# An LSTM whose input part arrives by accumulating DMAs: the bias under each step's tile written by ScalarE in place of a DMA

## The chip, the cores and the metric

The kernel runs on one core of one Trainium2 chip. The metric is the time of one execution on the device in microseconds, as the median over runs; lower is better. One further execution was taken with the hardware profiler on, and all rows of the profile come from that one.

## The reference

A batch of 32 sequences of 512 steps with 512 features goes through one LSTM layer of width 512, and the layer's output is added to its input. All numbers are fp32.

```python
xW = jnp.einsum('ntd,dg->ntg', x, Wx) + b          # 32 x 512 x 2048
def step(carry, xw_t):
    prev_h, prev_c = carry
    a = xw_t + prev_h @ Wh
    i, f, o = sigmoid(a[:, :H]), sigmoid(a[:, H:2*H]), sigmoid(a[:, 2*H:3*H])
    g = tanh(a[:, 3*H:])
    next_c = f * prev_c + i * g
    next_h = o * tanh(next_c)
    return (next_h, next_c), next_h
out = x + hs                                        # hs: all next_h
```

The bias `b` is a vector of 2048 numbers, one for each gate column, and it is not zero.

## The kernel before

The work has two halves that run side by side for nearly the whole time. The recurrence must go step by step: `h_part(k)` multiplies the state `ht` of the step before by `Wh` into two PSUM banks (`gates`), and `cell(k)` makes the new state from them. The input part `x @ Wx` doesn't depend on the recurrence, so its matmuls fill the time in which TensorE would wait for the cell.

**The input part.** The first 48 steps and the last 16 are made in simpler ways. The 448 steps between go in 14 blocks of 32. A block's product is made as 26 smaller products of sums of its rows with sums of blocks of `Wx` (the tables `A_OPS`, `B_OF`, `C_OPS`), and each of the 26 again as seven matmul groups (`product`). The sums of `Wx` lie in DRAM (`keep_a`, `keep_b`) and are fetched for each product into two rings of SBUF tiles, `wa` (3 buffers) and `wb` (4 buffers), by `fetch(v)`, lines 918 and 922; the rows of `x` for a block are fetched there too, four row loads of 512 KB for each block (line 214). ScalarE and VectorE move and add the PSUM results (`evacuate`, `finish_product`, lines 493 to 507, 617, 629, 645), and `store` (line 529) writes the finished blocks to DRAM in four pieces each, without the bias.

**A step's own tile.** For each step `t` from 8 to 495 a tile `xw[t]` of 128 x 512 floats (256 KB; a ring of four) is first filled with the bias, which stands in SBUF as `bias_sb` in the same shape. This is `fill_bias(t)`, line 715, and it is done by a plain DMA from SBUF to SBUF. Then `load_xw(t)`, line 719, issues a DMA on GpSimd that adds the stored product from DRAM onto the tile. Last, ScalarE copies the tile into the two banks ahead of the step's matmuls: `seed_first` (line 742) and `seed_last` (line 748).

**The order** is written out by hand, each engine's instructions in the order in which the program names them, and TensorE's, ScalarE's, VectorE's, GpSimd's and SyncE's queues each run in that order:

- In step `k` the loop first issues the load of residual rows (every second step), then `fill_bias(k + 4)` and `load_xw(k + 3)`.
- Then it puts `h_part(k)` on TensorE.
- Then come `evacuate`, the sums that are due, the matmuls `products(v)` with `v = k + 4`, and `fetch(v)`. So on ScalarE the copies of the evacuation stand ahead of the cell.
- Then comes `cell(k)`: ScalarE's three activations (lines 794 to 796), VectorE's products (797 to 799), ScalarE's tanh (800), VectorE's product and transpose (801, 802), which give `ht`. `put_step` adds the residual on GpSimd (line 855), and every second step SyncE issues the output's DMA (line 858).
- Last come the seeds for the steps after: `seed_first(k + 2)` and `seed_last(k + 1)`.

From step 469 on (`HALVES`), the cell and its matmuls go in two halves (`h_halves`, line 771, `cell_halves`, lines 816 to 842), with the same fill and load.

So SyncE's queue holds the fills, the fetches of `wa` and `wb`, the rows, the stores and the outputs, one behind the other. GpSimd's queue holds the accumulating DMAs and the residual's additions, one behind the other. A DMA that has to wait for something holds what stands behind it in its queue.

Of the kernel before, what the change touches and what calls it, by code (L numbers as in the profile page):

```python
# [40 lines left out]
END = HEAD + NSB * PER  # L41
# [131 lines left out]
def kernel(  # L173
# [9 lines left out]
    nc = tc.nc  # L183
# [19 lines left out]
    bias_sb = const.tile([P, G * P], F32, name="bias_sb")  # L203
# [5 lines left out]
    rows, xw, stored = {}, {}, {}  # L209
# [42 lines left out]
    def t_sums(i):  # L252
        w, t = raw[i], tt_[i]
        return [
            lambda: nc.vector.tensor_sub(t[:, 0::3], w[:, 1::2], w[:, 0:2]),
            lambda: nc.vector.tensor_sub(t[:, 1], w[:, 3], t[:, 0]),
            lambda: nc.vector.tensor_sub(t[:, 2], w[:, 2], t[:, 1]),
        ]
# [30 lines left out]
    def push_factors():  # L289
        v = nc.vector  # L290
        made, ops, done = {}, [], []

        def outer(n, how, a, b, part):
            if n not in made:
                made[n] = ring(n, f"make_{n}")

            def source(u):
                if part == 2:
                    return tt_[u] if u < 8 else made[u - 8][1]
                if u < 8:  # L300
                    return raw[u][:, 0:1] if part == 0 else raw[u][:, 2:4]
                return made[u - 8][0][:, 0:1] if part == 0 else made[u - 8][0][:, 1:3]

            (v.tensor_add if how == "add" else v.tensor_sub)(source(8 + n), source(a), source(b))

        for n in range(R):
            if streamed(n) and len(B_OF[n]) == 1:
                i = B_OF[n][0][0]
                ops.append((0, lambda n=n, i=i: keep(n, (raw[i][:, 0:1], raw[i][:, 2:4]), tt_[i])))
        for op in B_OPS:  # L310
            if isinstance(op, int):
                n = -1 - op
                ops.append((0, lambda n=n: keep(n, (made[n][0][:, 0:1], made[n][0][:, 1:3]), made[n][1])))
            else:
                for part, columns in ((0, C), (1, 2 * C), (2, 4 * C)):
                    ops.append((columns, lambda op=op, part=part: outer(*op, part)))
        for i, (columns, fn) in enumerate(ops):

            def go(fn=fn):
                fn()  # L320
                done.append(fn)

            push(2 + (START - 6) * i // len(ops), columns, go, lambda _, i=i: len(done) == i)
# [151 lines left out]
    def products(v):  # L475
        for late, ss in ((4, (4,)), (2, (7,)), (0, (1,)), (1, (6,)), (0, (5,)), (1, (5,)), (3, (2, 3))):
            job = jobs.get(v - late)
            for s in ss if job else ():
                if s != 5 or job.w5 == v:
                    product(job, s)  # L480
                if s == 4:
                    job.release()
# [183 lines left out]
    def direct(t, bank, qs=range(4), cols=slice(0, 512)):  # L666
        i, a = divmod(t, ROW)
        for q in qs:
            k, e = divmod(q, 2)
            for j in range(NJ):  # L670
                nc.tensor.matmul(  # L671
                    flat(bank)[j * B : (j + 1) * B, cols],
                    rows[i][:, a, q],
                    raw[NJ * k + j][:, 2 * e : 2 * e + 2].rearrange("p n c -> p (n c)")[:, cols],
                    start=q == 0,
                    stop=True,
                    skip_group_check=True,
                )

    def keep_direct(t, bank, room=None):  # L680
        if room is not None:
            xw[t] = room
        elif t < 4:
            xw[t] = upool.tile([P, G * P], F32, name=f"xw_{t}", tag="xw", bufs=4)
        else:
            xw[t] = node_free[t - 4].rearrange("p t e b -> p (t e b)")
        nc.vector.tensor_add(xw[t], flat(bank), bias_sb)
# [24 lines left out]

    def fill_bias(t):
        xw[t] = upool.tile([P, G * P], F32, name=f"xw_{t}", tag="xw", bufs=4)
        nc.sync.dma_start(out=xw[t], in_=bias_sb)

    def load_xw(t):
        i, a = divmod(t, ROW)
# [19 lines left out]
    def seed_first(t):  # L738
        if t == HALVES:
            seed_half(t, 0)  # L740
        elif t < HALVES:
            nc.scalar.copy(gates[t % 2][:, 0:IFG], xw[t][:, 0:IFG])  # L742

    def seed_last(t):
        if t == HALVES:
            seed_half(t, 1)
        elif t < HALVES:
            nc.scalar.copy(gates[(t + 1) % 2][:, IFG:], xw[t][:, IFG:])
# [31 lines left out]
    def x_last():  # L780
        state["x"] = work.tile([P, P], F32, name="x_last")
        nc.vector.transpose(state["x"], xr[T - 1][:, 1].rearrange("p q b -> p (q b)"))
# [91 lines left out]
    def prepare(v):  # L874

        job = jobs.get(v)
        ops = []
        if job is None or job.w >= START:
            return ops
        i, j = job.kind  # L880
        for k in range(2):
            if (i, k) not in head_sums:
                if (i, 0) not in head_sums:
                    both = spool.tile([P, 2, 4, 4, B], F32, name=f"s_h{i}", tag="sums", bufs=2)
                head_sums[i, k], more = inner_sums(block(raw_block(i, k)), both[:, k])
                ops += more
        job.factors = lambda s: [
            (left(block(raw_block(i, k)), s, head_sums[i, k]), raw_factor(NJ * k + j, s)) for k in range(2)
        ]
        job.finish = finish_unit(job, i, j)  # L890
        job.release = lambda: None
        return ops
# [45 lines left out]
    with tc.manual_schedule():  # L938
        warm = work.tile([P, G, P], F32, name="warm", tag="s")
        nc.scalar.activation(warm[:, 0], c_init, AF.Sigmoid)  # L940
        for m in range(3 * NJ):
            nc.tensor.matmul(
                pps[2][m % NJ * B : (m % NJ + 1) * B].rearrange("p n c -> p (n c)"),
                c_init[:, 0:B],
                c_init.unsqueeze(1).to_broadcast([P, 4, P]),
                start=True,
                stop=True,
            )
        nc.vector.transpose(
            bias_sb.rearrange("p (m l) -> p m l", l=B),  # L950
            bias_t.unsqueeze(2).to_broadcast([P, G * NJ, B]),
        )
        firsts = [gates[0], gates[1], pps[0], pps[1]]
        for q in range(4):
            for t in range(4):
                direct(t, firsts[t], (q,))
        for i in range(6):
            for op in t_sums(i):
                op()
        for op in prepare(0):  # L960
            op()
        products(0)
        for t in range(4):
            keep_direct(t, firsts[t])
        for i in range(6, 8):
            for op in t_sums(i):
                op()
        push_factors()
        for v, t in enumerate(range(4, ROW), 1):
            direct(t, gates[t % 2])  # L970
            for op in prepare(v):
                op()
            if v < 4:
                evacuate(v, 0)
            run_due(0, 2400)
            keep_direct(t, gates[t % 2])
            if v < 4:
                products(v)
                fetch(v)
        seed_first(0)  # L980
        seed_last(0)
        seed_first(1)

        for k in range(T):
            if k % 2 == 0 and k + 2 < T:
                load_residual(k + 2)
            if 2 * 4 - 4 <= k and k + 4 < END:
                fill_bias(k + 4)
            if 2 * 4 - 3 <= k and k + 3 < END:
                load_xw(k + 3)  # L990
            (h_part if k < HALVES else h_halves)(k)
            for m, v in enumerate(windows_of(k)):
                if v == START + 4:
                    assert len(due) == 0 or due[0][0] >= START
                    head_done()
                announce(v)
                room = HEAD_ROOM if v < START - 4 else ROOM if k < HALVES - 1 else HALF_ROOM
                run_due(v, room - evacuate(v, room))
                products(v)
                tail_products(v)  # L1000
                fetch(v)
                if k == T - 2:
                    x_last()
                if m == 0:
                    (cell if k < HALVES else cell_halves)(k)
                    seed_first(k + 2)
                    seed_last(k + 1)
                for op in prepare(v + 1):
                    op()
        assert not due  # L1010
# [51 lines left out]
```

## Time and profile before

| | us |
|---|---|
| median of 3 runs | 3136.03 (3135.21 to 3143.83) |
| the profiled execution, device time | 3151.96 |
| its span, first to last instruction | 3150.2 |
| TensorE busy in it | 3101.8 |
| VectorE, ScalarE, GpSimd busy | 2241.6, 1704.8, 824.3 |
| mean granted TensorE clock | 0.995 |

The profiled execution took 1.76 us beside its span, and it was 15.9 us longer than the median of the others. In the rows, PE is TensorE's matmuls and PEld its weight loads, ACT is ScalarE, DVE is VectorE, POOL is GpSimd and SPq is SyncE's queue, which only issues DMAs. `out<-in` names the tiles of an instruction; in a group's row stand, after the bar, its busy time and the mean of one instruction in ns, and after the next bar the time in which its engine sat idle just before it and what ended that. In a row of waits stand the total, the number of times and the longest. A row of the timeline begins with its start and its length, and ends, in brackets, with the idle time before it.

### The profile page before, as it was taken

How to read it: one execution, taken by the hardware profiler on the slowest of the kernel's cores; microseconds unless marked ns; L12 is line 12 of the kernel's file. 1: busy time of each engine (PE TensorE's matmuls, PEld its weight loads, DVE VectorE, ACT ScalarE, POOL GpSimd, SP SyncE). 2: the span in 40 equal slices, each digit the busy share in tenths (PEclk: the TensorE clock that was granted, in tenths of full speed). 3: DMA queues.
4: the chain of work that ended last, by engine and by line, in shares of the span. 5: the costliest groups of instructions: out<-in, count | busy, mean ns of one | idle time of the engine just before them, and what ended most of it. 6: DMA issues, size and time to landing. Idle time of an engine off the chain costs nothing.

```text
span 3150.2 us, 134152 instructions
## 1 busy us (share of the span) xinstructions
PE 3101.8 (98%) x56568; PEld 2007.1 (64%) x56568; DVE 2241.6 (71%) x6337; ACT 1704.8 (54%) x5186; POOL 824.3 (26%) x1001
## 2 busy tenths in 40 slices
PE   9999999999999999999999999999999999999999
PEld 4655566666666666666666566666666666666666
DVE  6636777777777777777777776777777777777644
ACT  2445555555555556555565555555555555555444
POOL 0112222232222222222222222222223223232320
PEclk9999999999999999999999999999999999999999
DMA  8868999999989999999999999999999999999840
GB/s 292 271 184 255 275 283 255 303 265 276 276 252 299 265 286 260 259 302 268 281 273 266 279 265 274 274 267 275 271 273 276 278 264 268 296 270 264 230 113 27
DMA packets 411563, 819.94 MB, mean 260 GB/s; under 512 B 52560, under 2 KB 121168, under 8 KB 410448
## 3 DMA queue, kind: packets, MB, share of 16 engines
q1 hardware_dynamic: 340544, 683.39, 64.1%
q0 software_dynamic: 70272, 127.96, 24.8%
q8 instruction: 445, 7.29, 0.9%
q14 instruction: 158, 1.29, 0.1%
q10 hardware_dynamic: 144, 0.01, 0.0%
HBM read 501.56 MB, written 181.67 MB: 217 GB/s over the span
## 4 chain that ended last, share of the span: by engine, by line
PE 88%; DMA 9%; ACT 1%; DVE 1%; issue 1%; SPq 0%; POOL 0%; POOLq 0%; DVEq 0%; ACTq 0%
PE gates L757 45%; PE pp L466 15%; PE acc L466 15%; PE p L466 5%; PE gates L771 5%; DMA xw<-xw 3%; DMA wb<-keep_b 3%; DMA xw<-bias_sb 2%; PE pp L671 1%; PE gates L671 1%; PE acc L671 1%; PE p L671 0%; ACT gates L742 0%; DMA xw<-slot_h 0%; DMA xw<-slot 0%
## 5 line engine op out<-in xcount | busy, mean ns | idle before, releaser
L757 PE MATMUL gates<-wh_sb,ht 128*32 128x384 f32 (+1 forms) x29952 | 1719.5, 380 | 4.0 <-DVE ht L802 2.6
L757 PEld LDWEIGHTS gates<-wh_sb,ht 128*32 128x32 f32 x29952 | 1034.9, 110 | 694.0 <-issue 595.1
L855 POOL TENSOR_TENSOR oc<-xr,ht 128x128 f32<-128x128 f32 x509 | 407.4, 800 | 1484.4 <-DVE ht L802 1336.3
L719 POOL DMA_DIRECT2D xw<-xw x488 | 432.3, 886 | 824.7 <-DMA xw<-bias_sb 231.3
L794 ACT ACTIVATE s<-gates 128x256 f32<-128x256 f32 x469 | 181.1, 386 | 533.7 <-PE gates L757 533.4
L466 PE MATMUL pp<-wb,nodes 128*32 128x256 f32 x3808 | 311.7, 383 | 0.0
L742 ACT COPY gates<-xw 128x384 f32<-128x384 f32 x465 | 220.7, 475 | 108.4 <-DMA xw<-xw 104.7
L507 DVE TENSOR_TENSOR pp<-acc,p 128x256 f32<-128x256 f32 x384 | 164.2, 428 | 152.7 <-ACT pp L506 152.5
L797 DVE TENSOR_TENSOR fc<-s,c 128x128 f32<-128x128 f32 x468 | 136.1, 291 | 191.5 <-ACT s L794 188.3
L801 DVE TENSOR_TENSOR fc<-s,ig 128x128 f32<-128x128 f32 x469 | 137.0, 292 | 176.5 <-ACT ig L800 176.5
L505 ACT COPY pp<-pu 128x512 f32<-128x512 f32 x384 | 231.2, 602 | 52.0 <-DVE t L629 19.4
L466 PE MATMUL acc<-wb,s 128*32 128x256 f32 x2576 | 209.4, 382 | 34.5 <-DMA wb<-keep_b 33.3
L796 ACT ACTIVATE s<-gates 128x128 f32<-128x128 f32 x469 | 130.5, 278 | 166.2 <-PE gates L757 166.0
L466 PE MATMUL acc<-wa,s 128*32 128x256 f32 x2576 | 211.0, 384 | 0.0
L466 PE MATMUL pp<-wb,s 128*32 128x256 f32 x2576 | 210.6, 383 | 0.0
L466 PE MATMUL p<-wa,s 128*32 128x256 f32 x2576 | 207.8, 379 | 0.0
L500 DVE TENSOR_TENSOR pu<-acc,p 128x256 f32<-128x256 f32 x384 | 159.6, 416 | 47.3 <-ACT p L497 34.4
L800 ACT ACTIVATE ig<-c 128x128 f32<-128x128 f32 x469 | 145.3, 310 | 84.6 <-DVE c L799 57.5
L506 ACT COPY pp<-acc 128x256 f32<-128x256 f32 x384 | 138.4, 361 | 91.0 <-DVE t L629 31.8
L802 DVE STREAM_TRANSPOSE ht<-fc 128x128 f32<-128x128 f32 x469 | 146.0, 311 | 49.7 <-DVE fc L801 0.9
L493 ACT COPY pu<-acc 128x256 f32<-128x256 f32 x384 | 143.1, 373 | 50.2 <-PE acc L466 50.2
L497 ACT COPY p<-p 128x256 f32<-128x256 f32 x384 | 146.1, 380 | 37.0 <-PE p L466 35.4
(218 smaller groups left out, 4515.6 us busy)
## 6 DMA issues: line engine op xcount, KB each, us to landing
wb<-keep_b SPq DMA_DIRECT2D x322, 512.0 KB, 6.8
xw<-bias_sb SPq DMA_DIRECT2D x488, 256.0 KB, 5.8
xw<-xw POOLq DMA_DIRECT2D x488, 256.0 KB, 6.2
wa<-keep_a SPq DMA_DIRECT2D x322, 384.0 KB, 6.0
xw<-t SPq DMA_DIRECT2D x348, 128.0 KB, 4.8
xw<-raw_sb SPq DMA_DIRECT2D x280, 128.0 KB, 4.3
xr<-in_x_dram SPq DMA_DIRECT2D x256, 128.0 KB, 5.0
out_dram<-oc SPq DMA_DIRECT2D x255, 128.0 KB, 4.4
```

What stands on the lines that cost most here:

```text
L466: nc.tensor.matmul(dst[t * B : (t + 1) * B], a[:, t], w, start=s in (1, 5) and m == 0, stop=True, skip_group_check=True,)
L497: nc.scalar.copy(job.p5, p5[:, 0])
L500: nc.vector.tensor_add(job.pu[:, 1], job.acc, job.p5)
L505: nc.scalar.copy(job.pp[0], job.pu)
L507: nc.vector.tensor_add(job.pp[1][:, 1], job.acc, job.p5)
L719: nc.gpsimd.dma_start(out=xw[t], in_=stored[i][a], accum_op=mybir.AluOpType.add)
L742: nc.scalar.copy(gates[t % 2][:, 0:IFG], xw[t][:, 0:IFG])
L757: nc.tensor.matmul(g[j * B : (j + 1) * B, cols], state["ht"][:, k, :], wh_sb[:, k, j, cols], start=False, stop=True, skip_group_check=True,)
L771: nc.tensor.matmul(bank_half(m)[j * B : (j + 1) * B], state["ht"][:, k, :], half(wh_sb[:, k, j], m), start=False, stop=True, skip_group_ch ...
L794: nc.scalar.activation(s[:, 0:2], g[:, 0:2], AF.Sigmoid)
L802: nc.vector.transpose(ht.rearrange("p q b -> p (q b)"), h)
L855: (nc.gpsimd if t < T - 3 else nc.vector).tensor_add(state["oc"][:, tt % 2], xr[t][:, tt % 2], ht)
```

## The change

The fill of a step's tile becomes a copy on ScalarE, and it moves in the program from the top of the step to just before the cell. The tile, its ring, the step for which it is made (`k + 4`) and the accumulating DMA stay.

```diff
     def fill_bias(t):
         xw[t] = upool.tile([P, G * P], F32, name=f"xw_{t}", tag="xw", bufs=4)
-        nc.sync.dma_start(out=xw[t], in_=bias_sb)
+        nc.scalar.copy(xw[t], bias_sb)
 
     def load_xw(t):
         i, a = divmod(t, ROW)
@@ -984,8 +984,6 @@
         for k in range(T):
             if k % 2 == 0 and k + 2 < T:
                 load_residual(k + 2)
-            if 2 * 4 - 4 <= k and k + 4 < END:
-                fill_bias(k + 4)
             if 2 * 4 - 3 <= k and k + 3 < END:
                 load_xw(k + 3)
             (h_part if k < HALVES else h_halves)(k)
@@ -1001,6 +999,8 @@
                 fetch(v)
                 if k == T - 2:
                     x_last()
+                if 2 * 4 - 4 <= k and k + 4 < END:
+                    fill_bias(k + 4)
                 if m == 0:
                     (cell if k < HALVES else cell_halves)(k)
                     seed_first(k + 2)
```

On ScalarE's queue the copy stands behind the last copy of the evacuation and in front of the first activation of the cell. SyncE's queue loses 488 issues. On the queues of GpSimd, VectorE and TensorE nothing moves.

## The prediction

> **What bounds the kernel now.** I read the page's engine shares first, then the groups of TensorE's instructions with the idle time before them, then who waited for whom.
>
> ```profile
> span 3150.2 us, 134152 instructions
> PE 3101.8 (98%) x56568; PEld 2007.1 (64%) x56568; DVE 2241.6 (71%) x6337; ACT 1704.8 (54%) x5186; POOL 824.3 (26%) x1001
> ...
> L757 PE MATMUL gates<-wh_sb,ht 128*32 128x384 f32 (+1 forms) x29952 | 1719.5, 380 | 4.0 <-DVE ht L802 2.6 <-ACT gates L748 1.4
> L466 PE MATMUL acc<-wb,s 128*32 128x256 f32 x2576 | 209.4, 382 | 34.5 <-DMA wb<-keep_b 33.3 <-DVE fc L801 1.2
> ...
> PE acc L466 <- DMA wb<-keep_b: 33.3, 14, 4.0
> ```
>
> TensorE is the bound: it is idle for 3150.2 - 3101.8 = 48.4 us, and no change to another engine can take more than that idle time and what follows from it. Of the 48.4 us, 33.3 are 14 waits for a block of `wb`, of 2.4 us on average (33.3 / 14), and 4.0 stand in front of the recurrence's matmuls. The question is then what makes `wb` late. One of the 14 waits, in the chain of work that ended last and in the timeline of the same stretch:
>
> ```profile
> 945.42 1.29 PE acc L466 x24
> 970.02 0.86 PE pp L466 x16
> 970.89 3.45 PE gates L757 x64
> 974.92 7.19 DMA wb<-keep_b
> 982.24 1.79 PE acc L466 x24
> 984.04 1.71 PE pp L466 x16
> 985.74 4.01 PE gates L757 x64
> ...
> 982.24 0.64 PE L466 MATMUL acc<-wb,s 128*32 128x256 f32 x8 [2.29 <-DMA wb<-keep_b]
> ```
>
> The block was issued at 974.92 and landed after 7.19 us. Who held it back is seen on the queues of GpSimd and SyncE just before:
>
> ```profile
> 964.36 0.88 POOL L719 DMA_DIRECT2D xw<-xw  x1 [6.10 <-ACT raw_sb L617]
> 964.97 0.77 POOL L855 TENSOR_TENSOR oc<-xr,ht 128x128 f32<-128x128 f32 x1
> ...
> 965.76 0.34 SPq L858 DMA_DIRECT2D out_dram<-oc  x1
> ...
> 974.92 1.30 SPq L922 DMA_DIRECT2D wb<-keep_b  x1
> ...
> POOL xw L719 <- DMA xw<-bias_sb: 231.3, 104, 8.3
> SPq L858 <- POOL oc L855: 776.5, 202, 9.4
> ```
>
> GpSimd sat for 6.10 us in front of an accumulating DMA. The releaser named there is ScalarE, but that DMA's wait is for the filled tile, and over the span 231.3 us of such waits are put down to the fill's DMA outright. So the residual's addition came late behind it, SyncE could issue the output only at 965.76, and the fetches stand behind that. Beside this loop, the DMA engines themselves have little room left in the long middle of the kernel:
>
> ```profile
> 340.00:2920.00 2580.00, 2541.44 (x46732) 1667.77 (x46724) 1926.00 (x5333) 1451.60 (x4297) 712.78 (x852) 0.99 0.95 274
> ...
> q1 hardware_dynamic: 340544, 683.39, 64.1%
> q0 software_dynamic: 70272, 127.96, 24.8%
> ...
> xw<-bias_sb SPq DMA_DIRECT2D x488, 256.0 KB, 5.8
> ```
>
> The last columns of the first row are the granted clock, the DMA engines' busy share (0.95) and GB/s. A transfer that gets late in a stage that is 95% full stays late until the burst (four row loads in each block of 32 steps) is over.
>
> **The fill's DMA removed.** It moved 488 x 0.262 MB = 128 MB of the 683 MB of its queue, so about 64.1% x 128 / 683 = 12 points of the DMA engines' time (an estimate by bytes). The middle goes from 0.95 to about 0.82. SyncE has one issue less in each step. Over the 40 us ahead of a stall, some seven steps, 7 x 0.262 = 1.8 MB fall out, at 274 GB/s 6.7 us of backlog: more than the longest wait (4.0).
>
> **The fill as a copy.** GpSimd's accumulating DMA of step k now waits for a copy that ScalarE has made in step k - 1 in front of the cell, and GpSimd gets to it only behind the residual's addition, which needs that cell's `ht`. So the wait is over before it begins, and the loop of GpSimd, output and fetch is cut. The accumulating DMA can only start earlier. With both, I take all 33.3 us of `wb` waits as gone, and the 4.0 us in front of the recurrence too, since they come from seeds and states that were late in the same bursts:
>
> ```profile
> ACT gates L742 <- DMA xw<-xw: 104.7, 72, 4.0
> ```
>
> **The clock.** A stall costs more than its idle time. In the chain above the matmuls behind the wait run slower than their like before it: 1.79 against 1.29, 1.71 against 0.86, 4.01 against 3.45, together 1.9 us. I took a window of 25 us around each stall; the column behind POOL's is the granted clock, and the first row is a stretch without a stall.
>
> ```profile
> 940.00:965.00 25.00, 25.00 (x470) 16.61 (x463) 17.63 (x54) 14.48 (x44) 5.47 (x9) 1.00 0.96 301
> 778.00:803.00 25.00, 21.40 (x380) 13.56 (x380) 15.53 (x43) 12.28 (x38) 5.82 (x7) 0.93 0.85 240
> ...
> 1940.00:1965.00 25.00, 21.52 (x363) 13.11 (x360) 15.20 (x41) 10.80 (x33) 5.77 (x7) 0.86 0.82 236
> ...
> 2526.00:2551.00 25.00, 22.33 (x402) 14.71 (x397) 16.56 (x46) 12.06 (x36) 6.35 (x8) 0.93 0.85 249
> ```
>
> Of these windows eight show a lower clock, seven 0.93 and one 0.86 (the first, the odd one and the last are shown). That is (7 x 0.07 + 0.14) x 25 = 15.8 us, and it goes with the stalls. The Trainium skill (TensorE: Matmul & The Clock Gate, section "Why this matters for your kernels") warns of gaps over about 3 us, since one whole idle window drops the clock; by that the stall of 2.29 us would have cost no clock, and if none did, the sum below would end at 3115. The trace has slow matmuls behind that very stall, so the measurement decides here.
>
> **ScalarE's 488 copies.** No row shows a copy from SBUF to SBUF. The nearest have one side in PSUM:
>
> ```profile
> L505 ACT COPY pp<-pu 128x512 f32<-128x512 f32 x384 | 231.2, 602 | 52.0 <-DVE t L629 19.4 <-DVE raw_sb L629 15.8 <-DVE slot_h L629 10.0
> L617 ACT COPY raw_sb<-pp 128x512 f32<-128x512 f32 x162 | 94.1, 583 | 56.3 <-PE pp L466 52.6 <-DMA wa<-keep_a 1.2 <-DMA xw<-t 1.2
> L794 ACT ACTIVATE s<-gates 128x256 f32<-128x256 f32 x469 | 181.1, 386 | 533.7 <-PE gates L757 533.4
> ...
> ACT s L794 <- PE gates L757: 533.4, 443, 3.1
> ...
> 1516.46 0.38 ACT L794 ACTIVATE s<-gates 128x256 f32<-128x256 f32 x1 [0.32 <-PE gates L757]
> 1518.47 0.31 DVE L802 STREAM_TRANSPOSE ht<-fc 128x128 f32<-128x128 f32 x1
> 1519.44 0.37 PEld L757 LDWEIGHTS gates<-wh_sb,ht 128*32 128x32 f32 x8
> ```
>
> I take 0.60 us for one (between 583 and 602 ns), so 488 x 0.60 = 293 us more work, and ScalarE goes to about 1998 us busy, 63%. What stands behind the copy on ScalarE is the cell; VectorE waits for that, and TensorE for VectorE's `ht`. But ScalarE sits idle at just that place, waiting for the gates: 533.7 / 469 = 1.14 us a step. A second cover stands behind it: in the step shown, `ht` is there at 1518.47 + 0.31 = 1518.78 and TensorE loads it at 1519.44, 0.66 us later, because the input part's matmuls run in between. In that step ScalarE's idle time is only 0.32, the cell would come 0.28 late, and the 0.66 swallow it. Even a step without any idle time would be 0.60 late at most, still under 0.66. So the cost on the path is nought. It can't be below nought, since nothing of ScalarE's work goes away. Its upper bound: 469 - 443 = 26 steps showed no such wait, and with a copy of twice 0.60 and 0.66 of cover they lose 26 x 0.54 = 14 us. I stay at nought because all but 26 steps have the first cover, and several of the 26 stand in stalled stretches.
>
> The Trainium skill (ScalarE: Activation LUTs, section "Step-by-step: what each stage is for") holds against this change that ScalarE writes PSUM faster than SBUF. The trace doesn't show a penalty: 583 ns with SBUF as the target, 602 with PSUM; and the same page's formula for an activation with immediate operands (section "What ACT_TABLE_LOAD costs") gives 186 + 0.833 x 512 = 613 ns, an estimate that no run here shows for this pair of memories.
>
> **The sum.** Against the profiled execution: 3151.96 - 33.3 - 4.0 - 15.8 + 0 = 3098.9, so 3099. How this stands to the median: the matmuls are the same in each run, so the median's 15.9 us less must be fewer or shorter stalls. Without stalls an ordinary run ends at the same place, 3099, which is 37 us (1.2%) under the median of 3136.03. What bounds next is TensorE's own stream.
>
> **The rivals.**
>
> *The stalls get shorter but stay.* The row loads and the stores of four pieces remain in SyncE's one queue, and a burst may fill the DMA engines still. For it: the stretch 940 to 965 moved 301 GB/s with the share at 0.96, and fills are only a part of that. Against it: 6.7 us of relief stand against waits of 2.4 on average. If half of the 53.1 us stays, the time is 3125 against the profiled execution and about 3118 against the median; I give it 3120.
>
> *The fills weren't the cause, and nothing changes:* `wb` would wait on its ring of four buffers or on the stores ahead of it. Then the time stays at 3136. Against it speaks the 6.10 us on GpSimd's queue.
>
> *ScalarE becomes the bound, and it is slower.* In-order ScalarE must do the copy between the evacuation and the cell. The two covers together are 1.14 + 0.66 = 1.80 us on the mean, and each microsecond beyond them costs 488 us. The loss passes the gain of 37 us from a copy of 1.80 + 37 / 488 = 1.88 us on; at 2.0 us it would be 3099 + 488 x 0.20 = 3197. A copy between two SBUF tiles would have to be three times the rows' price for that. That the copy itself waits is unlikely: its buffer was last read by a seed on the same queue a step earlier.
>
> **How the numbers follow.** Stalls gone 0.81, 3099; stalls halved 0.12, 3120; no change 0.03, 3136; slower 0.04, 3197. About 0.3% (9.4 us) is what a measurement of this kernel can tell from no change, so faster means under 3126.6: the first two cases, 0.93; same 0.03; slower 0.04. The range's low end is all of TensorE's idle time and the clock's loss gone: 3151.96 - 48.4 - 15.8 = 3088. The high end takes in the 14 us of uncovered copies (3113) and the halved stalls up to 3121.
>
> **What would show it.** In the profile after: the wait of PE for `wb` under 5 us, the mean clock near 1.00 at every block, DMA share in the middle near 0.82, the group of line 715 on ScalarE at 0.58 to 0.62 us with 488 instructions, the idle time in front of line 794 down from 1.14 to some 0.6 us a step, no wait of line 719 for a fill, and PE idle on `ht` at a few us. Wrong would be: `wb` waits above 15 us (first rival), or TensorE's idle time in front of line 757 above 20 us, released by `ht` (the last).

## The result and the profile after

| | before | after |
|---|---|---|
| median, us | 3142.17 (5 runs, 3135.21 to 3146.29) | 3092.00 (5 runs, 3091.51 to 3092.59) |
| profiled execution, device time | 3151.96 | 3091.51 |
| its span | 3150.2 | 3089.7 |
| TensorE busy / idle in the span | 3101.8 / 48.4 | 3080.0 / 9.7 |

The ratio after to before is 0.9845 (95% interval 0.9829 to 0.9861): 1.55% faster. It is also steadier: the five runs lie within 1.1 us, those of before within 11.1. The five runs of before are the three on which the prediction was made and two more, and the median of the five is some 6 us higher. The profiled execution of before is longer than any of the five, so its waits are on the high side for an ordinary run.

The page of the kernel after, its first lines and the groups that answer to those shown of before, the row of the page's queues for SyncE's DMAs, and, last, SyncE's wait for the residual's addition:

```profile
span 3089.7 us, 133411 instructions
PE 3080.0 (100%) x56568; PEld 2041.2 (66%) x56568; DVE 2240.1 (73%) x6337; ACT 1958.6 (63%) x5674; POOL 817.4 (26%) x1001
...
L757 PE MATMUL gates<-wh_sb,ht 128*32 128x384 f32 (+1 forms) x29952 | 1714.9, 379 | 0.0
L719 POOL DMA_DIRECT2D xw<-xw x488 | 428.8, 879 | 22.0 <-ACT pp L505 2.6
L794 ACT ACTIVATE s<-gates 128x256 f32<-128x256 f32 x469 | 180.2, 384 | 347.0 <-PE gates L757 336.3
L715 ACT COPY xw<-bias_sb 128x512 f32<-128x512 f32 x488 | 308.1, 631 | 0.0
L742 ACT COPY gates<-xw 128x384 f32<-128x384 f32 x465 | 219.9, 473 | 3.2 <-DVE nodes L687 3.0
L466 PE MATMUL acc<-wb,s 128*32 128x256 f32 x2576 | 206.8, 379 | 0.1
...
q1 hardware_dynamic: 270272, 555.43, 53.9%
...
SPq L858 <- POOL oc L855: 1051.6, 247, 10.2
```

TensorE's waits for `wb` are gone: the idle time in front of that group fell from 34.5 us to 0.1, that in front of the recurrence from 4.0 to 0.0. GpSimd's idle time in front of the accumulating DMA (line 719), 824.7 us before, is 22.0. SyncE's wait for the residual's addition, the next link of the loop in the prediction, didn't shrink: it grew from 776.5 us to 1051.6, with the stalls gone. So the size of that wait was no sign of lateness. ScalarE has 488 copies more, 308.1 us, and TensorE doesn't wait for them. What is left of TensorE's idle time, 9.7 us, lies at the start, in the last steps and at the end. The window of the long middle shows full TensorE (2539.93 of 2540), a clock of 1.00 and the DMA engines' share at 0.86:

```profile
340.00:2880.00 2540.00, 2539.93 (x47068) 1686.88 (x47064) 1938.15 (x5368) 1685.69 (x4760) 713.25 (x859) 1.00 0.86 237
```

The stretch whose stall the prediction showed, now in the timeline after: GpSimd's and SyncE's queues, and TensorE at the matmuls that had waited.

```profile
953.15 0.80 POOL L855 TENSOR_TENSOR oc<-xr,ht 128x128 f32<-128x128 f32 x1 [4.73 <-DVE ht L802]
953.91 0.89 POOL L719 DMA_DIRECT2D xw<-xw  x1
...
953.99 0.34 SPq L858 DMA_DIRECT2D out_dram<-oc  x1
955.26 2.61 SPq L529 DMA_DIRECT2D xw<-slot  x4
957.97 3.55 SPq L529 DMA_DIRECT2D xw<-raw_sb  x4
961.61 0.52 SPq L918 DMA_DIRECT2D wa<-keep_a  x1
962.18 1.10 SPq L922 DMA_DIRECT2D wb<-keep_b  x2
...
965.44 3.66 PE L757 MATMUL gates<-wh_sb,ht 128*32 128x384 f32 x64
968.89 0.64 PE L466 MATMUL acc<-wb,s 128*32 128x256 f32 x8
```

The same stretch before, with the times of the rows not shown there:

```profile
967.31 2.07 SPq L529 DMA_DIRECT2D xw<-slot  x4
971.28 2.82 SPq L529 DMA_DIRECT2D xw<-raw_sb  x4
974.54 0.34 SPq L918 DMA_DIRECT2D wa<-keep_a  x1
...
976.29 3.67 PE L757 MATMUL gates<-wh_sb,ht 128*32 128x384 f32 x64
```

Measured from the start of the recurrence's matmuls of that step, the output went out at 965.76 - 976.29 = -10.5 us before and at 953.99 - 965.44 = -11.5 after, so the loop over GpSimd gave 0.9 us. The two stores stood 1.9 us apart before (971.28 less the end of the first, 967.31 + 2.07) and 0.1 after (the profile puts the gap before down to the landing of a row load), which gave another 1.8, of which the second store's longer issue took back 0.7 (3.55 against 2.82). `wb` went out at -1.4 before and at -3.3 after, 1.9 us earlier. So in this instance the gap between the stores counted as much as the loop. One instance doesn't settle the shares; the runs below narrow them.

### The profile page after: what moved, and what is told of

Its sections match the earlier page's. It is cut to its first block, busy times and chain, and to the rows that moved or that the text cites. A ratio compares the mean times of both kernels' runs of the same rounds, so it can differ in the third digit from the quotient of the medians.

```text
span 3089.7 us, 133411 instructions
## 1 busy us (share of the span) xinstructions
PE 3080.0 (100%) x56568; PEld 2041.2 (66%) x56568; DVE 2240.1 (73%) x6337; ACT 1958.6 (63%) x5674; POOL 817.4 (26%) x1001
## 3 DMA queue, kind: packets, MB, share of 16 engines
q1 hardware_dynamic: 270272, 555.43, 53.9%
q0 software_dynamic: 70272, 127.96, 26.3%
## 4 chain that ended last, share of the span: by engine, by line
PE 99%; DVE 0%; DMA 0%; ACT 0%; issue 0%; SPq 0%; DVEq 0%
PE gates L757 52%; PE acc L466 17%; PE pp L466 17%; PE p L466 6%; PE gates L771 5%; PE pp L671 1%; PE gates L671 1%; PE acc L671 1%; PE p L671 0%; DMA raw_sb<-in_L_cond_Wx_dram 0%; DVE fc L822 0%; ACT s L816 0%; DVE fc L828 0%; DVE c L824 0%; ACT ig L837 0%
## 5 line engine op out<-in xcount | busy, mean ns | idle before, releaser
L794 ACT ACTIVATE s<-gates 128x256 f32<-128x256 f32 x469 | 180.2, 384 | 347.0 <-PE gates L757 336.3
L715 ACT COPY xw<-bias_sb 128x512 f32<-128x512 f32 x488 | 308.1, 631 | 0.0
```

Of the source, the lines that this page charges most:

```text
L715: nc.scalar.copy(xw[t], bias_sb)
L794: nc.scalar.activation(s[:, 0:2], g[:, 0:2], AF.Sigmoid)
```

## The experiments

Theory A says that the stalls came from the fill's bytes: with 12 points of the DMA engines' time gone, transfers and the issues behind them are no longer late. Theory B is the loop of the prediction: GpSimd waits for the fill, and the residual, the output and the fetches stand behind that. The prediction used both without shares. Three runs cut one without the other. The kernel before was run again beside each group of experiments, with medians of 3136.78 and 3140.36 us.

**The fill stays a DMA, one step earlier** (`dma_early`).

```diff
-            if 2 * 4 - 4 <= k and k + 4 < END:
+            if k == 2 * 4 - 4:
                 fill_bias(k + 4)
+            if 2 * 4 - 4 <= k and k + 5 < END:
+                fill_bias(k + 5)
...
-        xw[t] = upool.tile([P, G * P], F32, name=f"xw_{t}", tag="xw", bufs=4)
+        xw[t] = upool.tile([P, G * P], F32, name=f"xw_{t}", tag="xw", bufs=5)
...
-            job.pu = upool.tile([P, 2, C], F32, name=f"pu_{job.w}", tag="pu", bufs=4)
+            job.pu = upool.tile([P, 2, C], F32, name=f"pu_{job.w}", tag="pu", bufs=3)
```

> The fill stays a DMA of 256 KB on SyncE's queue, but is issued one step earlier (ring of five tiles; the ring of the evacuation's pu tiles goes from four to three for the room). The bytes and SyncE's issues stay those of before; GpSimd should find the tile filled. Theory A (room on the DMA engines: the 12 points that the fill takes make the transfers late): nothing much changes, 3130 to 3150 us, DMA share in the middle 0.95, waits for wb 25 us or more. Theory B (GpSimd's wait for the fill holds the residual's addition, that holds the output's issue on SyncE, and that the fetches): most of the gain comes, 3092 to 3105 us, waits for wb under 8 us, idle time in front of line 719 under 100 us (825 before).

Measured: 3131.38 us against 3136.78 before, ratio 0.9976 (0.9961 to 0.9991). Its groups of line 719 and of TensorE's waiting matmuls, and its window of the middle:

```profile
L719 POOL DMA_DIRECT2D xw<-xw x488 | 429.0, 879 | 55.1 <-DMA xw<-bias_sb 21.7 <-ACT pp L505 5.5 <-issue 3.1
L466 PE MATMUL acc<-wb,s 128*32 128x256 f32 x2576 | 207.8, 381 | 28.8 <-DMA wb<-keep_b 18.9 <-DVE nodes L401 6.4 <-DVE ht L802 3.1
...
340.00:2880.00 2540.00, 2511.18 (x46336) 1665.69 (x46332) 1906.02 (x5285) 1438.19 (x4259) 704.56 (x846) 1.00 0.94 276
```

GpSimd's wait is gone (55.1 us of idle time there, 824.7 before), the share is still 0.94, and 28.8 of the 34.5 us are still there. Cutting the loop alone brought a quarter of a per cent, with one `pu` buffer less, whose price was not measured. That speaks for A. Nor is it shown that these 5 us came by way of the output and the fetches: the idle time in front of the recurrence's matmuls (line 757) went from 4.0 us to 0.0 as well. The total of the waits for `wb` (18.9 us) lies between what the two theories gave.

**Less bytes, the loop kept** (`less_wa`).

```diff
-    PLACE = {1: (0, 0), 5: (0, 1), 6: (0, 2), 4: (1, 0), 7: (1, 1), 2: (1, 2), 3: (1, 3)}
+    PLACE = {1: (0, 0), 5: (0, 0), 6: (0, 0), 4: (1, 0), 7: (1, 1), 2: (1, 2), 3: (1, 3)}
...
-            nc.sync.dma_start(out=job.ring[0].rearrange("p n c -> p (n c)"), in_=kept[B_AT[job.kind[1]]][0])
+            nc.sync.dma_start(out=job.ring[0][:, 0], in_=kept[B_AT[job.kind[1]]][0][:, 0:C])
```

> The kernel before, with only the first third of each wa block fetched and used in three matmul groups (two thirds of wa's fetch are left out, so the sums are others; every matmul stays). This takes 322 x 256 KB off the DMA engines, two thirds of what the fills move, and leaves GpSimd's wait for the fill's DMA as it was. Theory A: most of the gain comes, 3092 to 3105 us, share in the middle about 0.87, waits for wb under 8 us. Theory B: the loop is still there, 3120 us or more, waits for wb 15 us or more; idle time in front of line 719 still several hundred us under both.

Measured: 3101.06 us, ratio 0.9874 (0.9856 to 0.9891).

```profile
L719 POOL DMA_DIRECT2D xw<-xw x488 | 431.0, 883 | 594.7 <-DMA xw<-bias_sb 146.1 <-ACT pp L506 62.9 <-DMA xr<-in_x_dram 57.7
L466 PE MATMUL acc<-wb,s 128*32 128x256 f32 x2576 | 207.1, 379 | 7.9 <-DMA wb<-keep_b 4.2 <-DVE ht L802 2.7 <-DVE c L799 1.0
...
340.00:2880.00 2540.00, 2532.05 (x46881) 1682.18 (x46877) 1931.44 (x5348) 1455.06 (x4307) 715.93 (x857) 1.00 0.90 248
```

GpSimd still sits 594.7 us in front of line 719 (824.7 before), SyncE issues as many DMAs as before, and yet TensorE's wait is down to 7.9 us. With bytes off the engines that are two thirds of the fill's, seven to eight tenths of the gain are there: (3136.78 - 3101.06) / (3142.17 - 3092.00) = 0.71 by the medians, and 0.80 with the 3136.78 measured beside it in place of 3142.17. A again; the share fell to 0.90, not to 0.87. Two things are less clean than the text before the run says. GpSimd's wait shrank by a quarter too, and the bytes left out are those of the fetch that stands just ahead of `wb` on SyncE's queue, so the same number of bytes of the fills may be worth less.

**The copy, and the bytes put back** (`copy_and_dma`).

```diff
+            if 2 * 4 - 4 <= k and k + 4 < END:
+                nc.sync.dma_start(out=dram.tile([P, G * P], F32, name=f"spill_{k}", tag="spill", bufs=8), in_=bias_sb)
             if 2 * 4 - 3 <= k and k + 3 < END:
                 load_xw(k + 3)
```

> The changed kernel, and at the fill's old place SyncE again issues a DMA of 256 KB from the bias tile, now to DRAM where nobody reads it (ring of eight). The bytes and the issues of before are back, GpSimd doesn't wait for them. Theory A (room on the DMA engines): the stalls come back nearly whole, 3125 to 3145 us, waits for wb over 15 us, share in the middle 0.94 or more. Theory B (GpSimd's wait): 3092 to 3100 us.

Measured: 3126.70 us against 3140.36 before, ratio 0.9956 (0.9941 to 0.9970). GpSimd hardly waits, and the stalls are back with a share of 0.95, as A had it. The profiled execution took 3135.19 us, the ten 3119.30 to 3135.19:

```profile
L719 POOL DMA_DIRECT2D xw<-xw x488 | 429.6, 880 | 20.1 <-issue 1.7 <-ACT pp L505 0.4
PE acc L466 <- DMA wb<-keep_b: 22.2, 10, 4.2
...
q1 hardware_dynamic: 340544, 683.39, 63.9%
...
340.00:2880.00 2540.00, 2511.37 (x46300) 1657.31 (x46296) 1905.80 (x5283) 1660.25 (x4679) 703.01 (x845) 1.00 0.95 276
```

The bytes go to DRAM and not to SBUF here, but they load the DMA engines as the fills did (63.9% of their time for SyncE's queue, 64.1% before). The run answers to `dma_early` from the other side: with the bytes of before and the loop cut, the gain is 5 to 14 us; with the bytes off and most of the loop kept, 36. What isn't bytes is the smaller part.

There is a third way for the fill to do harm, which neither theory names: on SyncE's queue it waits for the tile to be free, that is for the seed of line 748, and holds the fetches behind it. First before, then in `less_wa`:

```profile
SPq L715 <- ACT gates L748: 125.6, 80, 5.9
```

```profile
SPq L715 <- ACT gates L748: 150.6, 78, 5.9
```

`less_wa` keeps this wait and still has its 36 us, so it isn't the main cause. `copy_and_dma` is without it, since nobody reads what its DMA writes. So the 14 us there may hold some of it beside the loop's; the 5 us of `dma_early`, where the wait still stands at 112.7, can hold little.

**Half of the tiles by copy** (`copy_half`): the copy in odd steps, the DMA at the old place in even ones.

```diff
+            if 2 * 4 - 4 <= k and k + 4 < END and k % 2 == 0:
+                fill_bias(k + 4, nc.sync.dma_start)
...
-                if 2 * 4 - 4 <= k and k + 4 < END:
+                if 2 * 4 - 4 <= k and k + 4 < END and k % 2 == 1:
                     fill_bias(k + 4)
```

> Every second tile (odd steps) is filled by ScalarE's copy in front of the cell, the others by the DMA at the old place. Half of the bytes go, and half of GpSimd's waits. Theory A: a relief of 6 points; the backlog of a burst shrinks by 3.3 us against waits of 2.4 us on average, so most of the gain comes, 3092 to 3105 us. Theory B: half of the waits in front of line 719 remain and with them about half of the stalls, 3110 to 3125 us.

Measured: 3104.39 us, ratio 0.9889 (0.9871 to 0.9906), at the upper end of what A gave. Its group of TensorE's waiting matmuls and its window of the middle:

```profile
L466 PE MATMUL acc<-wb,s 128*32 128x256 f32 x2576 | 206.8, 379 | 11.0 <-DMA wb<-keep_b 9.3 <-DVE fc L801 1.2 <-DVE ig L798 0.4
...
340.00:2880.00 2540.00, 2528.95 (x46785) 1676.27 (x46781) 1925.70 (x5339) 1562.23 (x4512) 712.26 (x853) 1.00 0.90 257
```

The share is 0.90 and 9.3 us of waits for `wb` are left. Half of the fills bring (3136.78 - 3104.39) / 50.2 = 65% of the gain, or 72% with 3136.78 in place of 3142.17. That is more than half, so the first points of room look to be worth more than the last; the run also halves GpSimd's wait (402.2 us in front of line 719), so it doesn't part the two theories by itself.

**The DMA at the copy's place** (`dma_at_cell`).

```diff
-        nc.scalar.copy(xw[t], bias_sb)
+        nc.sync.dma_start(out=xw[t], in_=bias_sb)
```

> The changed kernel with the copy turned back into the DMA on SyncE, at the copy's new place in the program (behind the fetches, in front of the cell). Bytes and issues are those of before; GpSimd now gets to the accumulating DMA some 2.5 us after the issue of a fill that takes 5.8 us to land, so it waits about 3 us in every step, 1500 us in all, and every residual addition and output is late. Theory A: 3130 to 3150 us as before. Theory B: slower than before, 3150 to 3250 us, waits for wb over 50 us.

Measured: 3379.65 us, ratio 1.0769 (1.0744 to 1.0794), far beyond what either theory gave. The reason is another wait, seen in its groups of ScalarE, GpSimd and TensorE:

```profile
L742 ACT COPY gates<-xw 128x384 f32<-128x384 f32 x465 | 222.3, 478 | 576.7 <-DMA xw<-xw 572.6 <-DVE nodes L687 3.0
L719 POOL DMA_DIRECT2D xw<-xw x488 | 433.8, 889 | 2017.0 <-DMA xw<-bias_sb 648.6 <-ACT ig L800 232.6 <-ACT s L795 182.6
L757 PE MATMUL gates<-wh_sb,ht 128*32 128x384 f32 (+1 forms) x29952 | 1734.2, 381 | 169.2 <-ACT gates L748 87.0 <-DVE ht L802 80.8 <-issue 0.5
L466 PE MATMUL acc<-wb,s 128*32 128x256 f32 x2576 | 209.1, 387 | 14.3 <-DVE pu L500 14.2
```

GpSimd waits 2017 us, the accumulating DMAs land after the seeds want them (572.6 us of ScalarE's time), and the recurrence waits for its seed: 169.2 of TensorE's 3378.6 - 3158.2 = 220.4 us of idle time stand in front of line 757. TensorE waits 14.3 us in front of the `wb` matmuls, none of it put down to `wb` itself. So the place in front of the cell suits a fill that is done in 0.63 us and not one that lands 5.8 us after its issue (the median of before).

**The copy at the old place** (`copy_on_top`): only the fill's engine is changed, the program's order is that of before.

```diff
-        nc.sync.dma_start(out=xw[t], in_=bias_sb)
+        nc.scalar.copy(xw[t], bias_sb)
```

> ScalarE's copy at the fill's old place in the program, at the top of the step, so on ScalarE ahead of the evacuation's copies and not behind them. The DMA engines are relieved as in the changed kernel. If the place in front of the cell is what makes the copy free (the idle time in front of line 794 takes it), this one is slower, 3100 to 3130 us, with TensorE waiting for evacuations or for ht. If any place in the step will do, since the evacuation's copies end well ahead of the gates, it is 3090 to 3096 us.

Measured: 3093.40 us, ratio 0.9850 (0.9830 to 0.9870), beside 0.9845 for the changed kernel: no difference that can be told. The copies cost as much, but take their time elsewhere:

```profile
L794 ACT ACTIVATE s<-gates 128x256 f32<-128x256 f32 x469 | 181.1, 386 | 503.1 <-PE gates L757 503.0
L715 ACT COPY xw<-bias_sb 128x512 f32<-128x512 f32 x488 | 302.5, 620 | 14.7
L497 ACT COPY p<-p 128x256 f32<-128x256 f32 x384 | 147.0, 383 | 7.5 <-PE p L466 7.5
```

ScalarE still waits 503.1 us for the gates (347.0 after, 533.7 before). Part of the copies went into waits of the evacuation (line 497, 7.5 us of idle time against 37.0 before). The half of the change that moves the fill isn't needed.

**Copies of twice and three times the length** (`copy_twice`, shown, and `copy_thrice` with one line more).

```diff
         nc.scalar.copy(xw[t], bias_sb)
+        nc.scalar.copy(xw[t], bias_sb)
```

> The changed kernel with each copy made twice, one behind the other, about 1.2 us a step. By the prediction's mean covers (1.14 us in front of the gates and 0.66 us in front of the state's use, together 1.80) only the steps without the first cover lose, 14 us at most: 3092 to 3106 us. The rival: the covers differ from step to step and the mean says little, since ScalarE's other waits in the step can't be filled; then many steps run over, 3106 to 3140 us.

> Each copy made three times, about 1.8 us a step. The prediction's means put the break-even with the kernel before at 1.88 us a copy, so it should still be under 3142 us, 3100 to 3135. The rival (covers that differ, and lateness that is carried from step to step): 3150 to 3350 us, with TensorE idle in front of line 757 for ht.

Measured: 3104.96 us for two (ratio 0.9888, 0.9867 to 0.9908), 3196.52 for three (1.0179, 1.0154 to 1.0203). The recurrence's matmuls and their idle time, for two copies with ScalarE's wait for the gates, then for three:

```profile
L758 PE MATMUL gates<-wh_sb,ht 128*32 128x384 f32 (+1 forms) x29952 | 1714.0, 379 | 4.0 <-DVE ht L803 3.8 <-ACT raw_sb L617 0.2
...
ACT s L795 <- PE gates L758: 131.4, 233, 1.9
```

```profile
L759 PE MATMUL gates<-wh_sb,ht 128*32 128x384 f32 (+1 forms) x29952 | 1714.3, 380 | 62.5 <-DVE ht L804 54.8 <-ACT raw_sb L617 1.4 <-ACT slot L617 0.2
L715 ACT COPY xw<-bias_sb 128x512 f32<-128x512 f32 x488 | 308.8, 633 | 0.0
L716 ACT COPY xw<-bias_sb 128x512 f32<-128x512 f32 x488 | 301.9, 619 | 15.4
L717 ACT COPY xw<-bias_sb 128x512 f32<-128x512 f32 x488 | 301.8, 618 | 15.6
```

Two copies cost 13 us, within the prediction's bound of 14, but that the number fits is luck. The bound counted 26 steps without a wait for the gates and let each lose 0.54 us. In the run 469 - 233 = 236 steps are without that wait, and most of them lose nothing all the same. Measured from the start of a step's recurrence matmuls to that of the next, 60 of 468 steps are more than 0.05 us longer than in the changed kernel, by 0.2 us on the mean. Three take (308.8 + 301.9 + 301.8) / 488 = 1.87 us a step, just under the prediction's break-even of 1.88, and make the kernel 56 us slower than before and 105 slower than after. The waits in front of the recurrence name `ht`: ScalarE's lateness reaches the recurrence, as the last rival had it, only earlier than its price said. By the same measure 235 steps are longer, 103 us together, and the other 233 keep their time; the long ones recur in each block of 32 steps.

## Why the prediction was right, step by step

**The time and the sign.** 3099 was forecast within 3088 to 3121, and 3092.0 was measured; the likeliest case, all stalls gone, is the one that came.

**The terms of the sum**, against the profiled executions: 3151.96 - 3091.51 = 60.5 us where 53.1 were forecast. TensorE's idle time fell by 48.4 - 9.7 = 38.7 us; the terms for `wb` and for the recurrence gave 33.3 + 4.0 = 37.3. Its busy time fell by 3101.8 - 3080.0 = 21.8 us where the clock's term gave 15.8. The mean clock went from 0.995 to 1.000, which is 0.005 x 3150 = 16 us, so that term holds; 6 us of busy time beyond it are what was left out. They needn't be the clock: with two and three copies the clock is 1.00 throughout, and TensorE's busy time still grows with its idle time, from 3080.0 to 3088.7 and 3120.7 us beside 14.0 and 74.3 us idle. A likely cause, not shown by a run: the last matmul before each wait counts its whole 380 ns as busy, while in a full stream the next one runs beside it (64 in 3.67 us above, 57 ns each). The medians fell by 50 us where 37 were forecast; 6 of the 13 are the higher median of before.

**The bytes and the loop.** The step "with both, I take all 33.3 us" was right. GpSimd's wait is gone (22.0 us) and so are the bytes. But the argument led with the loop over GpSimd, and the runs show that all but the bytes is worth 5 to 14 us and the bytes most of the rest. The 776.5 us of SyncE's wait for the residual, shown there as a link of the loop, are 1051.6 in the faster kernel. The time couldn't tell the two apart, since the change takes both away: on this point the forecast was right without the shares being known. The share of the middle, forecast as 0.82, was 0.86: the fill's bytes are gone as counted (683.39 MB to 555.43), but the same remaining work now runs in less time, which makes about 1.5 points of the four ((3150.2 / 3089.7 - 1) of some 78). The rest is open; the accumulating DMAs, unchanged in bytes, went from 24.8% to 26.3%, a point more than the shorter time gives.

**The wait on ScalarE.** The step of 0.60 us a copy was 5% low (631 ns). The idle time in front of the gates fell from 1.14 to 347.0 / 469 = 0.74 us a step, where some 0.6 were expected: it gave up 186.7 of the 308.1 us. Another 105 us of idle time went from the seed's wait for the accumulating DMA, 108.4 us before and 3.2 after, which the prediction hadn't counted as room. The wait for the gates is left in fewer steps than the bound took, 348 of 469 after and 443 before:

```profile
ACT s L794 <- PE gates L757: 336.3, 348, 2.6
```

So 121 steps, and not 26, had to live on the second cover, and they could: TensorE's idle time in front of the recurrence is 0.0. The cost on the path was nought, as said.

**The rivals.** Stalls that stay in part are what `copy_half` and `less_wa` show at 0.90 of share. "The fills weren't the cause" is out. The slower rival's mechanism is right and its price wrong: "1.14 + 0.66 = 1.80 us on the mean" can't be spent as a mean: with 1.87 us a step about half of the steps lost nothing and the other half 0.44 us each, so idle time left over in one step was no cover for another. Whether a late step also makes the next one late, no run shows by itself. The step that failed is the break-even from two means; three copies at 1.87 us lost 105 us where that sum gave 0.07 x 488 = 34.

## What to carry to other kernels

A plain fill of a tile by DMA isn't free because no engine makes it: here the DMA engines were at 0.95, its bytes made other transfers late, and giving them to an engine with idle time paid even though that engine got 300 us more work. Before crediting a chain of waits that the profile shows, test it apart from the bytes: here it was in the trace, its first link was cut, and most of the gain came from elsewhere. The total of a wait says little about harm: one link of that chain waited longer in the faster kernel. Idle time in front of a wait is cover step by step; a mean over the steps says what the first 0.6 us cost and not where it ends.

## What the runs showed of the hardware

A stall of a few microseconds can cost more than itself. These are the windows of before around the stall of 2.29 us that the prediction showed, and around one of 2.82 us:

```profile
972.00:997.00 25.00, 22.71 (x400) 14.73 (x396) 16.95 (x48) 12.25 (x38) 5.76 (x7) 0.93 0.86 249
...
1555.00:1580.00 25.00, 22.18 (x416) 14.55 (x412) 16.74 (x46) 12.77 (x38) 6.13 (x7) 1.00 0.96 266
```

In the first TensorE was idle for 25.00 - 22.71 = 2.29 us, and the granted clock was 0.93, another 0.07 x 25 = 1.75 us. Eight windows of before had a lower clock. The second, with more idle time, kept 1.00, so a stall of this length doesn't always lower it; no run shows what makes the difference. The whole middle of the kernel after is at 1.00. The accumulating DMAs used the DMA engines about twice as long as the plain ones of SyncE's queue, byte for byte: their queue moved 127.96 MB in 24.8% of their time, SyncE's 683.39 MB in 64.1%, which is 12.0% for as many bytes. A copy on ScalarE from SBUF to SBUF (128 x 512, fp32) took 631 ns in front of the cell and 620 at the old place, against 583 from PSUM to SBUF and 602 from SBUF to PSUM, so in these rows PSUM on either side was the shorter way. For the target that is what the Trainium skill holds (ScalarE: Activation LUTs, section "Step-by-step: what each stage is for"), and here it was 18 to 29 ns.
